# Storing layer 1's rows from SyncE in rank order and gathering them by rank in the batch norm's stage

## The chip, the cores and the metric

The kernel runs on one core of a Trainium2 chip. The metric is the device time of one execution in microseconds (us), from the first to the last instruction. Five engines work side by side, each on its own in-order list of instructions: TensorE (PE, matrix products), VectorE (DVE), ScalarE (ACT), GpSimd (POOL, which here does little but issue indirect DMAs) and SyncE (SP, which issues the plain DMAs).

## The reference

A graph of N = 2708 nodes with 128 features each, and a sparse weighted adjacency `adj` (about 0.6% of the entries and the diagonal), go through four layers. Each is `x = layernorm(x + layer(x, adj))`:

```
L0: (adj.T @ x) / column sums of adj
L1: s, d = x @ Ws.T, x @ Wd.T
    agg[i] = sum_j adj[i, j] * gelu(s[i] + d[j] + b)
    layernorm(gelu([x, agg] @ U.T + b) + x) * w + b
L2: h = adj @ (x @ W) + b;  batch norm over the nodes;  leaky relu
L3: 4 heads of GATv2 attention over adj, then a projection
```

What matters here: the result of layer 1, one row per node, is needed twice. Times W it goes into layer 2's product, and as it is it is added to layer 2's output after the batch norm (the residual).

## The kernel before

Layer 0 is one pass over `adj` in 22 blocks of 128 rows (the last has 20). The same pass finds each row's nonzero entries, counts them, and **ranks** the nodes by that count within two groups of blocks. From then on layer 1 works in rank order: a block holds 128 nodes of neighbouring rank, so that all need about the same number of neighbours (`CAPS`, 30 down to 8). Two tables translate: `rank[p, b]` is the rank of node 128b+p, and `perm[p, b]` is the node of rank 128b+p.

**Layer 1** takes the 22 blocks in the order `TURNS` (0 to 18, 21, 19, 20). For a block, `messages(b)` lets POOL gather one neighbour row per node and neighbour from `d_dram` (`gather`, L247; 368 gathers in all) into a `msg` tile of up to 8 neighbours (five such tiles in turn). DVE adds `s` (L896), ACT takes the gelu (L899), and DVE weighs and sums (L884) into `parts`. `update(b)` then runs a chain through PE, ACT and DVE (two layer norms) that ends in the block's finished rows `x_n` (written by `normalised`, L321). `x_n` goes two ways: it is transposed on PE (L937) and multiplied by W into `xw` (L941, L942), and it is **scattered** by `perm` to `x2_dram` in the nodes' natural order (L936, issued by POOL through `scatter`, L255; each waits also for the one before it, since all write one tensor).

In the first half of this stage, beside it, PE transposes `adj` (L969, L976) through SP into `at_dram`. In the second half, beside it, **layer 2** runs: `layer2(k)` gathers 128 whole rows of `at_dram` by `perm` (1.4 MB, POOL, `at_rows`) and multiplies them with `xw` of the block into six accumulators (L1018). Layer 2's output comes out in the nodes' natural order.

**The batch norm's stage** follows. It loads layer 1's rows `x2` from `x2_dram` (two plain loads on SP, L1103 and L1104), adds a shift to the accumulators (`hb`, L1129), sums the squares over the nodes with matmuls by ones (`ps_v`, L1132), makes `bn_scale` of that, and then per group of up to four blocks scales (L1185, L1186, L1187), adds `x2` (L1190), normalises into `x_nat` (L321), scatters these rows by `rank` to `x3_dram` (POOL, 22 scatters), and forms layer 3's table `t2_dram` with PE, ACT and SP (L1213 to L1232). Beside it `masks(g)` makes constants for layer 3: POOL writes index patterns (`jrow` L1147, `row_of` L1155, `start` L1157) and DVE turns them into `first`, `copies`, `alike`, `mask` and `same` (L1159 to L1179); three of the seven kinds stand in the program before the scaling, four after it.

**Layer 3** gathers rows of `t2_dram` (400 gathers on POOL) and works on them to the end.

The order of each engine's instructions is worked out when the program is built, by a planner that runs the program with estimated costs and, for each engine, takes the earliest instruction of the program that is ready; only layer 0's DVE work and layer 3's PE, DVE and ACT work have their order written out by hand. The planner also places every wait. The SBUF space of `x2` is free only when layer 2's last product has been read.

Of the kernel before, what the change touches and what calls it, by code (L numbers as in the profile page):

```python
# [15 lines left out]
P = 128  # L16
N = 2708
D = 128
NFULL = N // P
NREM = N - NFULL * P  # L20
NBLK = NFULL + 1
# [40 lines left out]
BLOCKS = [(b * P, min(P, N - b * P)) for b in range(NBLK)]  # L62
# [23 lines left out]
def gnn_resnorm_kernel(  # L86
# [21 lines left out]
    nc = tc.nc  # L108
# [108 lines left out]
    x2_dram = tables.tile([NBLK * P, D], FP, name="x2_dram")  # L217
# [6 lines left out]
    perm = keep.tile([P, NBLK], I32, name="perm")  # L224
# [7 lines left out]
    rank = keep.tile([P, NBLK], I32, name="rank")  # L232
# [9 lines left out]
    def natural(dram, b0, b1):  # L242

        return dram[b0 * P : b1 * P, :].rearrange("(b p) w -> p b w", p=P)

    def gather(dst, table, index):
        nc.gpsimd.indirect_dma_start(  # L247
            out=dst,
            out_offset=None,
            in_=table[0:N, :],  # L250
            in_offset=bass.IndirectOffsetOnAxis(ap=index, axis=0),
        )

    def scatter(table, index, rows):
        return nc.gpsimd.indirect_dma_start(  # L255
            out=table,
            out_offset=bass.IndirectOffsetOnAxis(ap=index, axis=0),
            in_=rows,
            in_offset=None,
        ).ins  # L260
# [35 lines left out]
    def deviation(small, n, count, h, sums, newton=True):  # L296


        var = small.tile([P, 4], FP, name="ln_var")
        junk = small.tile([P, D], BF, name="ln_junk")  # L300
        nc.vector.tensor_scalar(sums, sums, -1.0 / D, None, ALU.mult)
        for j in range(count):
            nc.scalar.activation(
                junk[0:n], h[:, j, :], AF.Square, bias=sums[:, j : j + 1],
                accum_out=var[0:n, j : j + 1],
            )
        v = var[0:n, 0:count]
        nc.vector.tensor_scalar(v, v, 1.0 / D, EPS, ALU.mult, ALU.add)
        if newton:
            for _ in rsqrt(small, n, count, v):  # L310
                pass
        else:
            nc.scalar.activation(v, v, AF.Sqrt)
            nc.vector.reciprocal(v, v)
        return var

    def normalised(small, n, count, h, sums, dst, newton=True):

        var = deviation(small, n, count, h, sums, newton)
        for j in range(count):  # L320
            nc.vector.tensor_scalar(  # L321
                dst[:, j, :], h[:, j, :], sums[:, j : j + 1], var[0:n, j : j + 1],
                ALU.add, ALU.mult,
            )
# [12 lines left out]
    with ExitStack() as layer:  # L337
# [568 lines left out]
        def update(b, x_s, x_st, parts):  # L906
            n = BLOCKS[b][1]
            tp = tail_ps.tile([P, 512], FP, name="tail")
            for i in range(2):
                nc.tensor.matmul(  # L910
                    tp[:, 0:n], lhsT=parts[0:n, i, :], rhs=ident[0:n, 0:n],
                    start=(i == 0), stop=(i == 1),
                )
            x_b = mine.tile([P, D], FP, name="x_b")
            nc.vector.tensor_tensor(x_b[0:n], x_s[0:n, 1, :], lnb[0:n], ALU.add)
            agg_t = mine.tile([P, P], FP, name="agg_t")
            nc.scalar.copy(agg_t[:, 0:n], tp[:, 0:n])
            pn = tp[0:n, P : 2 * P]
            nc.tensor.matmul(pn, lhsT=x_st[:, 0:n], rhs=u1_t, start=True, stop=False)
            nc.tensor.matmul(pn, lhsT=ones[0:1, 0:n], rhs=updb[0:1, :], start=False, stop=False)  # L920
            nc.tensor.matmul(pn, lhsT=agg_t[:, 0:n], rhs=u2_t, start=False, stop=True)
            new = mine.tile([P, 1, D], FP, name="new")
            x_n = mine.tile([P, 1, D], FP, name="x_n")
            sums = mine.tile([P, 2], FP, name="sums1")
            h, s0, s1 = new[0:n, 0, :], sums[0:n, 0:1], sums[0:n, 1:2]
            nc.scalar.activation(h, pn, AF.Gelu)
            nc.vector.scalar_tensor_tensor(
                h, h, 1.0, x_s[0:n, 1, :], ALU.mult, ALU.add, accum_out=s0
            )
            rstd = deviation(mine, n, 1, new[0:n], s0)  # L930
            nc.vector.scalar_tensor_tensor(h, h, s0, lnw[0:n], ALU.add, ALU.mult)
            nc.vector.scalar_tensor_tensor(
                h, h, rstd[0:n, 0:1], x_b[0:n], ALU.mult, ALU.add, accum_out=s1
            )
            normalised(mine, n, 1, new[0:n], s1, x_n[0:n])
            scatter(x2_dram, perm[0:n, b : b + 1], x_n[0:n, 0, :])  # L936
            nc.tensor.transpose(tp[:, 256 : 256 + n], x_n[0:n, 0, :], ident[0:n, 0:n])  # L937
            x_nt = mine.tile([P, P], FP, name="x_nt")
            nc.scalar.copy(x_nt[:, 0:n], tp[:, 256 : 256 + n])
            px = tp[0:n, 384:512]  # L940
            nc.tensor.matmul(px, lhsT=x_nt[:, 0:n], rhs=w2_l2, start=True, stop=True)  # L941
            nc.scalar.copy(xw[0:n, b, :], px)  # L942
# [92 lines left out]
        for i, b in enumerate(TURNS):  # L1035
# [10 lines left out]
            for _ in range(2 if i < 1 else 1):  # L1046
                if left:
# [6 lines left out]
                    if e == NBLK - 1:  # L1054
                        run(place(NBLK - 2, NBLK, lists(NBLK - 2, NBLK)))
            update(b, x_s, x_st, agg)
            if second and i:
                own_scatter(*second.pop(0))
# [39 lines left out]
    with ExitStack() as layer:  # L1098
# [1 line left out]
        small = layer.enter_context(tc.tile_pool(name="bn_small", bufs=2))  # L1100
        hb = work.tile([P, NBLK, D], FP, name="hb")
        x2 = work.tile([P, NBLK, D], FP, name="x2")
        nc.sync.dma_start(x2[:, 0:NFULL, :], natural(x2_dram, 0, NFULL))  # L1103
        nc.sync.dma_start(x2[0:NREM, NFULL, :], x2_dram[NFULL * P : N, :])  # L1104
        a_all = keep.tile([P, HEADS, D], FP, name="a_all")
        nc.scalar.dma_start(a_all, att.partition_broadcast(P))
        w1_sb = keep.tile([P, HEADS, D], FP, name="w1_s")
# [989 lines left out]
```

## Time and profile before

| | us |
|---|---|
| time, median of 3 runs | 1930.35 |
| the runs | 1926.28, 1930.35, 1936.67 |
| the profiled execution: its span | 1936.7 |
| layer 0 and the lists, about | 0 to 300 |
| layer 1, transposes beside it | 300 to 660 |
| layer 1, layer 2 beside it | 660 to 1033 |
| batch norm's stage | 1033 to 1117 |
| layer 3 | 1117 to 1937 |

The profiled execution's span, 1936.7 us, agrees with the slowest of the three runs, so it stands 6.3 us above the median. Busy over the whole span are PE 64%, DVE 60%, POOL 46% and ACT 40%. In the lines of the profile, "POOL L255 x_dram<-x_n,perm" is layer 1's scatter (buffer numbers are left out of names, so `x2_dram` and `x3_dram` both read `x_dram`), "L247" is a gather, and `[9.24 <-DVE x_n L321]` says that the engine stood idle for 9.24 us before this instruction and what ended the wait. "issue" is a wait that the profile doesn't explain by another engine.

### The profile page before, as it was taken

How to read it: one execution, taken by the hardware profiler on the slowest of the kernel's cores; microseconds unless marked ns; L12 is line 12 of the kernel's file. 1: busy time of each engine (PE TensorE's matmuls, PEld its weight loads, DVE VectorE, ACT ScalarE, POOL GpSimd, SP SyncE). 2: the span in 40 equal slices, each digit the busy share in tenths (PEclk: the TensorE clock that was granted, in tenths of full speed). 3: DMA queues.
4: the chain of work that ended last, by engine and by line, in shares of the span. 5: the costliest groups of instructions: out<-in, count | busy, mean ns of one | idle time of the engine just before them, and what ended most of it. 6: DMA issues, size and time to landing. Idle time of an engine off the chain costs nothing. (4 is left out here: it accounts for less than half of the span.)

```text
span 1936.7 us, 23643 instructions
## 1 busy us (share of the span) xinstructions
PE 1240.9 (64%) x5771; PEld 864.1 (45%) x5771; DVE 1166.6 (60%) x4895; ACT 776.5 (40%) x3156; POOL 892.8 (46%) x1003
## 2 busy tenths in 40 slices
PE   7974313353446553554673748888788788878885
PEld 7973212242334442554663314544444444444444
DVE  8997445675635423433447417777678677676774
ACT  3565345543324210211122415555455555445553
POOL 1004654445653366445331474655555556555430
PEclk9986555555555576776676756676676777666675
DMA  8642645666545525223231574865566655756540
GB/s 283 238 150 79 131 140 165 174 183 174 141 103 142 177 43 160 95 92 140 79 113 44 167 239 131 212 190 163 145 196 183 182 166 160 191 150 192 150 115 7
DMA packets 167676, 289.63 MB, mean 150 GB/s; under 512 B 49600, under 2 KB 121502, under 8 KB 160429
## 3 DMA queue, kind: packets, MB, share of 16 engines
q0 software_dynamic: 60496, 190.77, 34.4%
q1 hardware_dynamic: 99489, 92.57, 15.6%
q10 hardware_dynamic: 7544, 4.69, 1.0%
q8 instruction: 48, 0.79, 0.2%
q14 instruction: 99, 0.81, 0.1%
HBM read 242.51 MB, written 45.36 MB: 149 GB/s over the span
## 5 line engine op out<-in xcount | busy, mean ns | idle before, releaser
L247 POOL DMA_INDIRECT g<-t_dram,idx x400 | 398.6, 996 | 316.0 <-issue 178.9
L247 POOL DMA_INDIRECT msg<-d_dram,idx x368 | 348.6, 947 | 260.2 <-issue 164.8
L1389 ACT ACTIVATE sum_junk<-g 126x128 bf16<-126x128 f32 (+3 forms) x1024 | 301.3, 296 | 142.4 <-issue 59.8
L1358 PE MATMUL z<-x,copies 32*126 32x512 f32 (+3 forms) x800 | 221.3, 944 | 65.8 <-DVE g L1555 45.0
L969 PE MATMUL pt_a<-ident,rows 128*128 128x128 f32 (+2 forms) x475 | 114.1, 395 | 144.4 <-ACT at_sb L974 79.5
L1555 DVE TENSOR_TENSOR g<-g,z 126x1536 f32<-126x1536 f32 (+3 forms) x100 | 175.0, 1750 | 44.0 <-DMA g<-t_dram,idx 15.3
L1018 PE MATMUL acc<-x_nat,at_rows 128*128 128x128 f32 (+2 forms) x968 | 160.7, 326 | 52.3 <-DMA at_rows<-at_dram,perm 26.5
L1389 ACT ACTIVATION_READ_ACCUMULATOR sum_junk<-g 126x1 f32 (+3 forms) x1024 | 191.6, 187 | 0.0
L1018 PEld LDWEIGHTS acc<-x_nat,at_rows 128*128 128x128 f32 (+2 forms) x968 | 144.1, 232 | 65.5 <-issue 38.7
L1363 PE MATMUL z<-g,ident 126*126 126x512 f32 (+3 forms) x200 | 169.3, 941 | 0.7 <-issue 0.7
L1435 PE MATMUL po_s<-wm,g 126*128 126x24 f32 (+6 forms) x800 | 128.6, 316 | 58.5 <-DVE wm L1422 56.2
L1435 PEld LDWEIGHTS po_s<-wm,g 126*128 126x128 f32 (+3 forms) x800 | 124.8, 243 | 75.6 <-DVE wm L1422 67.9
L969 PEld LDWEIGHTS pt_a<-ident,rows 128*128 128x128 f32 (+2 forms) x475 | 82.9, 205 | 167.5 <-ACT at_sb L974 92.8
L884 DVE SCALAR_TENSOR_TENSOR own<-msg,ls,own 128x128 f32<-128x128 f32 (+1 forms) x302 | 105.6, 350 | 85.4 <-ACT msg L899 28.5
L1381 DVE SCALAR_TENSOR_TENSOR g<-g,a_ps 126x1536 f32<-126x1536 f32 (+6 forms) x100 | 151.0, 1510 | 0.0
L420 PE MATMUL acc<-x_nat,rows 128*128 128x129 f32 (+3 forms) x1012 | 128.5, 288 | 26.0 <-DMA rows<-in_adj_dram 14.9
L420 PEld LDWEIGHTS acc<-x_nat,rows 128*128 128x128 f32 (+2 forms) x1012 | 123.0, 198 | 31.2 <-DMA rows<-in_adj_dram 16.0
L1358 PEld LDWEIGHTS z<-x,copies 32*126 32x126 f32 (+3 forms) x800 | 67.8, 261 | 100.3 <-issue 46.5
L899 ACT ACTIVATE msg<-msg 128x896 f32<-128x896 f32 (+4 forms) x55 | 50.4, 917 | 132.9 <-DVE msg L896 92.1
L1373 DVE SCALAR_TENSOR_TENSOR g<-z,a 126x128 f32<-126x128 f32 (+3 forms) x400 | 91.9, 285 | 19.5 <-remote 9.2
L445 DVE FIND_INDEX8 ci<-cv,rows 128x8 uint32<-128x247 f32 (+2 forms) x242 | 98.7, 408 | 0.0
L1363 PEld LDWEIGHTS z<-g,ident 126*126 126x126 f32 (+3 forms) x200 | 42.0, 263 | 124.3 <-issue 117.3
(302 smaller groups left out, 2132.2 us busy)
## 6 DMA issues: line engine op xcount, KB each, us to landing
rows<-in_adj_dram SPq DMA_DIRECT2D x34, 1354.0 KB
at_dram<-at_sb SPq DMA_DIRECT2D x105, 256.0 KB
g<-t_dram,idx POOLq DMA_INDIRECT x400
msg<-d_dram,idx POOLq DMA_INDIRECT x368
t_dram<-t_row SPq DMA_DIRECT2D x21, 256.0 KB
x_s<-dx_dram SPq DMA_DIRECT2D x21, 128.0 KB
at_dram<-at_sb SPq DMA_DIRECT2D x21, 64.0 KB
t_dram<-x_nat SPq DMA_DIRECT2D x5, 256.0 KB
```

What stands on the lines that cost most here:

```text
L247: nc.gpsimd.indirect_dma_start(out=dst, out_offset=None, in_=table[0:N, :], in_offset=bass.IndirectOffsetOnAxis(ap=index, axis=0),)
L420: nc.tensor.matmul(accs0[k][0:m, c0 : c0 + f1 - f0], lhsT=rows[0:n, j0 : j0 + m], rhs=x_nat[0:n, b, f0:f1], start=k not in started, stop=( ...
L445: nc.vector.max_index(out=ci[0:n, at], in_max=cv[0:n, at], in_values=rows[0:n, c0 : c0 + cw])
L884: nc.vector.scalar_tensor_tensor(to, m, v, last, ALU.mult, ALU.add)
L969: nc.tensor.transpose(pt[0:m, j, 0:n], rows[0:n, c0 : c0 + m], ident[0:n, 0:n])
L1018: nc.tensor.matmul(accs2[ib // 4][0:m, (ib % 4) * D : (ib % 4 + 1) * D], lhsT=at[0:n, i0 : i0 + m], rhs=xw[0:n, b, :], start=(k == 0 and i ...
L1358: nc.tensor.matmul(z3[0:e, r, :] if r < 3 else z1[0:e], lhsT=copies[g][rows, j, :], rhs=own[b][1][rows, :], start=True, stop=r < 3, skip_g ...
L1363: nc.tensor.matmul(z1[0:e], lhsT=ident[0:e, 0:e], rhs=g4[0:e, 3, 0:HD], start=False, stop=True, skip_group_check=True,)
L1381: nc.vector.scalar_tensor_tensor(z, z, 0.0, a_ps[0:e].unsqueeze(1).to_broadcast((e, count, HD)), ALU.max, ALU.mult)
L1389: nc.scalar.activation(junk[0:e], g4[0:e, r, hd * D : (hd + 1) * D], AF.Identity, accum_out=sc[0:e, r, hd : hd + 1],)
L1435: nc.tensor.matmul(po[:, p0 * HEADS : (p0 + g) * HEADS], lhsT=g4s[i][0:e, r, HD : HD + D], rhs=wm[0:e, 4 * i + r, :, :], start=True, stop= ...
L1555: nc.vector.tensor_tensor(z, z, z3[0:e], ALU.add)
```

## The change

The 22 scatters of `x_n` are replaced by 22 plain stores from SP, block by block, so `x2_dram` holds the rows in rank order. In the batch norm's stage the two plain loads are replaced by 22 gathers on POOL, one per block of 128 nodes, that fetch by `rank`. What is computed is the same, and so are the bytes that are moved.

```diff
@@ update(b) in layer 1
             normalised(mine, n, 1, new[0:n], s1, x_n[0:n])
-            scatter(x2_dram, perm[0:n, b : b + 1], x_n[0:n, 0, :])
+            nc.sync.dma_start(x2_dram[b * P : b * P + n, :], x_n[0:n, 0, :])
             nc.tensor.transpose(tp[:, 256 : 256 + n], x_n[0:n, 0, :], ident[0:n, 0:n])
@@ the batch norm's stage
         hb = work.tile([P, NBLK, D], FP, name="hb")
         x2 = work.tile([P, NBLK, D], FP, name="x2")
-        nc.sync.dma_start(x2[:, 0:NFULL, :], natural(x2_dram, 0, NFULL))
-        nc.sync.dma_start(x2[0:NREM, NFULL, :], x2_dram[NFULL * P : N, :])
+        for b in range(NBLK):
+            n = BLOCKS[b][1]
+            gather(x2[0:n, b, :], x2_dram, rank[0:n, b : b + 1])
```

## The prediction

> **What bounds the kernel now.** I read the busy time by stage first, since the change touches two stages only.
>
> ```profile
> core 0: us, PE busy (x) PEld busy (x) DVE busy (x) ACT busy (x) POOL busy (x), PEclk, DMA share, GB/s
> 300.00:660.00 360.00, 160.99 (x650) 124.77 (x650) 201.60 (x1013) 141.41 (x297) 174.26 (x183) 0.55 0.56 147
> 660.00:1033.00 373.00, 213.30 (x1250) 185.60 (x1250) 143.55 (x613) 59.15 (x162) 169.75 (x180) 0.70 0.33 109
> 1033.00:1062.00 29.00, 7.55 (x48) 7.01 (x46) 26.44 (x90) 9.32 (x26) 1.89 (x11) 0.67 0.20 57
> 1062.00:1117.00 55.00, 39.00 (x114) 20.54 (x113) 26.13 (x144) 22.39 (x63) 23.50 (x27) 0.75 0.51 163
> ```
>
> No engine fills layer 1 (300 to 1033); its second half leans on PE (213 of 373). From 1033 to 1062 DVE is the bound (26.4 of 29), from 1062 on PE's chain. Second view: POOL's waits, 660 to 1033.
>
> ```profile
> POOL x_dram L255 <- DVE x_n L321: 67.1, 6, 16.5
> ...
> POOL x_dram L255 <- DVE own L884: 47.5, 5, 14.1
> POOL x_dram L255 <- DVE spread L618: 15.1, 1, 15.1
> ```
>
> So the scatter holds POOL for 129.7 us in 12 of the last blocks (from 300 to 660 never over 0.3 us). A hold costs only if something behind it is late. Message gathers are early: block 18's ran from 874 to 909 and DVE took the first at 926. Layer 2's `at_rows` gathers are not. Third view, the timelines of POOL and PE around 720:
>
> ```profile
> 717.83 1.00 POOL L255 DMA_INDIRECT x_dram<-x_n,perm  x1 [9.24 <-DVE x_n L321]
> 719.13 0.96 POOL L247 DMA_INDIRECT msg<-d_dram,idx  x1 [0.30 <-issue]
> ...
> 726.64 0.94 POOL L247 DMA_INDIRECT at_rows<-at_dram,perm  x1 [0.30 <-issue]
> ...
> 735.62 4.63 PE L1018 MATMUL acc<-x_nat,at_rows 128*128 128x128 f32 x25 [12.10 <-DMA at_rows<-at_dram,perm]
> ```
>
> POOL stands 9.24 us for `x_n`, then issues six message gathers, then `at_rows`; PE stands 12.10 us for it. Fourth view, DVE and POOL in the batch norm's stage:
>
> ```profile
> 1033.12 0.13 POOL L1147 IOTA jrow<- 128x8 int32 x1 [8.18 <-PE acc L1018]
> ...
> 1033.35 0.22 DVE L1159 TENSOR_SCALAR first<-jrow,in 128x8 f32<-128x8 int32 x1
> ...
> 1042.75 0.29 DVE L1142 TENSOR_SCALAR bn_scale<-ps_v 128x128 f32<-128x128 f32 x1 [2.49 <-PE ps_v L1132]
> ...
> 1044.14 1.87 DVE L1166 TENSOR_REDUCE alike<-copies 128x128 f32<-128x1024 f32 x1
> ...
> 1051.35 0.69 DVE L1185 TENSOR_TENSOR hb<-hb,bn_scale 128x512 f32<-128x512 f32 x1
> ```
>
> POOL's patterns are ready at once, so DVE makes masks ahead of the scaling, on the path.
>
> **Part 1, the scatters leave POOL.** Each took 1.00 us and 0.30 to the next, 22 x 1.30 = 28.6 us. In the first half messages are gathered some 30 us ahead of use (block 5's end at 442, DVE starts it at 473), and five message tiles stop POOL, not the scatter: 0. In the second half what counts is PE's waits for `at_rows`, 26.5 us in four: 4.95 before the first scatter that holds, which stays; 12.10 at 736; 6.18 at 811; 3.30 at 979. The scatters ahead of the last three held POOL 9.24, 3.20 and 15.09 us. Hold and scatter gone, each can shrink by the smaller of the two: 9.24 + 1.30 = 10.5, 3.20 + 1.30 = 4.5, and 3.3, together 18.3 us. PE is in order and carries this half, so a wait removed moves what follows; but chains through ACT and DVE can absorb some, and message tiles can stop POOL instead. Bounds 0 and 18.3; I take two thirds, 12 us, nearer the upper end because most of it is the one wait at 736.
>
> **Part 2, the stores on SP.** A 128 KB row load on SP (L857) mostly took 0.3 to 0.5 us to issue: 22 x 0.4 = 9 us on a queue that is empty for long stretches after 660, so 0 there. A store waits for `x_n`, and behind it in the first half stand `at_dram` stores; late ones hold the three `at_sb` tiles, ACT's copies behind them, and with ACT the gelu. ACT already waits 27.4 us on these stores (25 times, 4.7 at most) in layer 1. In the second half only `own_row` loads stand behind, which wait for a later step of the same chain. Bounds: 0, and 27 if those waits doubled; I take +2, since the planner puts the store where it expects `x_n`.
>
> **Part 3, 22 gathers in the batch norm's stage.** They can't start before 1033.1, when `x2`'s space comes free (the old load issued then too). At the message gathers' spacing, 0.94 + 0.30 = 1.25 us, POOL is held 22 x 1.25 = 27.5 us, to 1060.6. An indirect transfer is complete about 2.6 us after its start (two scatters of lists that wait for each other stand 2.6 apart, 463.29 and 465.88). So block b lands near 1033.1 + 1.25b + 2.6: block 3 at 1039.5, 11 at 1049.5, 21 at 1062. DVE added them at 1056.5, 1065.3 and 1088.9; 8 us earlier that would still be 1048, 1057 and 1081. All in time: the gathers themselves cost 0, and the removed loads gain 0, being hidden in the same way.
> A rule speaks against this part. The Trainium skill's "DMA: Bandwidth & Descriptors", section "Rules for kernel authors", says to join many small transfers into a large one, and its section on the anatomy of a GpSimd DMA gives about 2.0 us plus bytes over 436 GB/s for each. As an estimate from that page, one after another, 22 x 2.15 = 47 us would end at 1080, just at the last row's need. The 1.25 us spacing in this trace shows that they overlap, so the rows decide, and by the page too the sum would hardly change.
>
> What stands behind the gathers on POOL does move: the five patterns of 1033.1 to 1033.8 run at 1060.6 (the planner takes earlier instructions first, and the gathers are earlier). DVE's three masks, 11.5 us between 1033 and 1062 (L1162 4.19, L1166 4.70, the small ones 2.6), can't run there. If the planner fills in the scaling, it starts when the scale is ready: ACT's root ends at 1043.8, then 0.94 and 0.28 on DVE, 1045.05 instead of 1051.35, 6.3 us sooner; two further mask steps (1.7 us) before the first `x_nat` at 1061.4 make it 8 at most. I take -6. The 11.5 us go into 1062 to 1117, where DVE has 55 - 26 = 29 free, so they cost 0; without that cover they would cost 11.5. The 22 `x3_dram` scatters start at 1062 and end at 1096 now, then POOL idles 12.9 us to 1108.8: gathers to 1061 leave them where they are.
>
> One cost is unseen: `ps_v`'s 44 products (7.2 us, to 1042.7, on the path) will run beside indirect DMAs. Beside them PE's pace varies: 24 products in 2.84 us at 901, but 55 from 684 to 713 with POOL busy for 18.8 us, against 30 in 6 us right after, with POOL still. At 0.53 us each, 44 would take 23 us: +16; at the first pace 0. I take +3, nearer the low end, since at 684 the granted clock was low too (0.62).
>
> **Sum** against the profiled 1936.7: -12 + 2 - 6 + 3 = -13, 0.67%. On the median, 1930.35 x 0.9933 = 1917.
>
> **Rivals.**
> *The gain is absorbed.* Block times in layer 1 are set by PE, ACT and DVE handing over to one another, the `at_rows` waits become waits for message tiles, and part 3 balances. For it: ACT and DVE show waits of up to 27 us there that no scatter explains. Against it: the 12.1 us wait is plain. -13 + 12 = -1: about 1929.
> *Masks stall DVE (slower).* If the planner keeps a mask step where it stands on DVE, DVE waits in order for POOL's patterns behind 22 gathers. Place: `first<-jrow`, third on DVE at 1033.35, ahead of `hb`; price 1060.6 - 1033.3 = 27; if only those between 1042.95 and 1045.9 stay, 1060.6 - 1043 = 18. It decides as soon as any mask instruction stands ahead of the first L1185 on DVE. For it: they stand there now. Against it: the planner knows that POOL is held. Without part 3's -6: -12 + 2 + 3 + 18 to 27 = +11 to +20: 1941 to 1950.
> *POOL's freedom is worth more.* A quarter of the 129.7 us of holds, 32, instead of 12: 1897. Against it: message gathers are early.
>
> **How the numbers follow.** Forecast 0.45, absorbed 0.20, masks stall 0.25, more 0.10. The forecast's own range is 1904 (18.3 and 8 gained, neither +2 nor +3) to 1928 (half of part 1's, `ps_v` at +8). The range over the cases is 1893 to 1946, which cuts the ends of the outer two. About 0.5%, 10 us, is what this measurement can tell from no change. Faster by that: most of the forecast and all of "more", 0.50. Slower: the masks and a little of costlier SP waits or `ps_v`, 0.28. The rest 0.22.
>
> **What would show it.** Right: no x_dram<-x_n on POOL; PE's `at_rows` wait near 736 gone, layer 1 ending some 10 us sooner; 22 gathers back to back on POOL at the stage's start, L1185 about 12 us into it and no mask ahead of it; masks after 1062. Wrong: the stage still ending 84 us after its start or later, DVE idle with POOL's pattern as releaser; `ps_v` stretched over 10 us; SP waits on `x_n` with ACT's `at_sb` waits grown; layer 1 as long as before.

## The result, and the profile after

The changed kernel takes 1941.37 us (median of 20 runs, 1931.4 to 1956.09) against 1930.24 us of the kernel before (20 runs): a ratio of 1.0058, 95% interval 1.0041 to 1.0076. It is slower by 11 us. The profiled execution has a span of 1941.6 us against 1936.7. One thing has to be known for the numbers further down: the kernel before took 1917.47 us beside the first group of experiments and 1602.52 and 1601.93 beside the second and third, so ratios are compared within a group only.

Below, "the stage" starts when DVE writes `bn_mean` (end of layer 1). Four marks are counted from there: the first `x_nat` written, the last `t_row` copied, layer 3's first gather (POOL), and layer 3's first product on `g` (DVE). Behind the changed line, line numbers of the changed kernel are one higher than before: L1186 is the scaling that was L1185, L1160 is `first`, L1163 `copies`.

The first view is busy time by window, as before (length, then PE, PEld, DVE, ACT, POOL):

```profile
core 0: us, PE busy (x) PEld busy (x) DVE busy (x) ACT busy (x) POOL busy (x), PEclk, DMA share, GB/s
660.00:1024.00 364.00, 220.21 (x1202) 188.68 (x1202) 136.13 (x587) 56.46 (x158) 148.22 (x157) 0.69 0.30 95
1024.00:1053.00 29.00, 6.00 (x47) 5.35 (x46) 8.91 (x20) 5.34 (x9) 22.20 (x24) 0.68 0.21 57
1053.00:1130.00 77.00, 35.79 (x115) 19.07 (x115) 44.72 (x212) 26.48 (x81) 28.18 (x40) 0.74 0.38 119
```

Layer 1 ends 8.9 us earlier (1024.15, was 1033.07). PE's chain there no longer shows the wait of 12.10 us: in the stretch where PE stood (723.5 to 735.6) it now computes (its blocks come some 20 us sooner there), and over the span its group of `acc` waits 6.7 us for `at_rows` (26.5 before). The first line is from PE's timeline, the second from the groups of PE (busy, mean ns, idle before and what ended it):

```profile
724.45 7.81 PE L1018 MATMUL acc<-x_nat,at_rows 128*128 128x128 f32 x54
```

```profile
L1018 PE MATMUL acc<-x_nat,at_rows 128*128 128x128 f32 x882 | 151.9, 333 | 17.7 <-issue 10.4 <-DMA at_rows<-at_dram,perm 6.7 <-ACT x_nat L942 0.4
```

In the first 29 us of the stage DVE now works 8.9 us, where it worked 26.4; POOL is the one busy engine. The timeline of POOL and DVE in that stretch (start, duration, idle time before in brackets):

```profile
1024.38 0.95 POOL L247 DMA_INDIRECT x<-x_dram,rank  x1 [78.04 <-PE pw L1092]
...
1051.97 0.90 POOL L247 DMA_INDIRECT x<-x_dram,rank  x1 [0.30 <-issue]
1052.90 0.15 POOL L1148 IOTA jrow<- 128x8 int32 x1
```

```profile
1034.63 0.69 DVE L1186 TENSOR_TENSOR hb<-hb,bn_scale 128x512 f32<-128x512 f32 x1
1053.09 0.23 DVE L1160 TENSOR_SCALAR first<-jrow,in 128x8 f32<-128x8 int32 x1 [17.76 <-issue]
...
1064.05 0.69 DVE L1186 TENSOR_TENSOR hb<-hb,bn_scale 128x512 f32<-128x512 f32 x1
...
1069.57 1.11 DVE L321 TENSOR_SCALAR x_nat<-hb,sums,ln_var 128x128 f32<-128x128 f32 x4
```

The 22 gathers run back to back from 1024.38 to 1052.87. DVE issues one scaling, 10.5 us into the stage, and then stands 17.76 us. Its next instruction is the first mask step, which reads `jrow`, and POOL makes `jrow` at 1052.90, behind the last gather. The masks of three kinds then run ahead of nearly all of the quads' steps, and the first `x_nat` is written 45.4 us into the stage (28.4 before). The bracket only says "issue"; that POOL is the releaser follows from the times here, and three later runs name it. PE, which needs `x_nat`, stands 37.77 us:

```profile
1069.97 1.24 PE L1214 MATMUL pt_x<-ident,x_nat 128*128 128x128 f32 x4 [37.77 <-DVE x_nat L321]
...
1135.66 1.75 DVE L1556 TENSOR_TENSOR g<-g,z 128x1536 f32<-128x1536 f32 x1 [2.92 <-PE z L1359]
```

Layer 3's first product on `g` follows 111.5 us after the stage's start, 91.9 before. The balance of the two profiles: 8.9 us won in layer 1, 19.6 lost in the stage, 5.8 won in layer 3 (805.9 against 811.7, where the program is the same); -8.9 + 19.6 - 5.8 = +4.9 = 1941.6 - 1936.7. The medians differ by 11.1; the profiled execution of the kernel before, at 1936.7, is slower than its median. A difference of 6 us between two single profiles thus proves nothing by itself.

### The profile page after: what moved, and what is told of

The parts are those of the page before. It is cut to its first block, busy times and chain, and to the rows that moved or that the text cites. A ratio compares the mean times of both kernels' runs of the same rounds, so it can differ in the third digit from the quotient of the medians.

```text
span 1941.6 us, 23697 instructions
## 1 busy us (share of the span) xinstructions
PE 1238.7 (64%) x5771; PEld 864.5 (45%) x5771; DVE 1165.8 (60%) x4895; ACT 774.2 (40%) x3156; POOL 895.8 (46%) x1003
## 5 line engine op out<-in xcount | busy, mean ns | idle before, releaser
L1359 PE MATMUL z<-x,copies 32*126 32x512 f32 (+3 forms) x800 | 212.5, 910 | 53.8 <-DVE g L1556 32.8
L1556 DVE TENSOR_TENSOR g<-g,z 126x1536 f32<-126x1536 f32 (+3 forms) x100 | 175.0, 1750 | 34.0 <-remote 19.9
L1018 PE MATMUL acc<-x_nat,at_rows 128*128 128x128 f32 (+2 forms) x968 | 169.5, 335 | 17.7 <-issue 10.4
L1018 PEld LDWEIGHTS acc<-x_nat,at_rows 128*128 128x128 f32 (+2 forms) x968 | 150.6, 239 | 32.6 <-issue 27.2
L420 PE MATMUL acc<-x_nat,rows 128*128 128x129 f32 (+3 forms) x1012 | 129.5, 289 | 26.5 <-DMA rows<-in_adj_dram 15.5
L1359 PEld LDWEIGHTS z<-x,copies 32*126 32x126 f32 (+3 forms) x800 | 63.9, 251 | 86.4 <-issue 46.1
L1374 DVE SCALAR_TENSOR_TENSOR g<-z,a 126x128 f32<-126x128 f32 (+3 forms) x400 | 91.9, 286 | 17.2 <-issue 13.1
L450 DVE MAX8 cv<-rows 128x8 f32<-128x247 f32 (+2 forms) x242 | 95.6, 401 | 2.4 <-POOL rows L410 2.4
```

The costliest lines, as they stand in the source:

```text
L420: nc.tensor.matmul(accs0[k][0:m, c0 : c0 + f1 - f0], lhsT=rows[0:n, j0 : j0 + m], rhs=x_nat[0:n, b, f0:f1], start=k not in started, stop=( ...
L1018: nc.tensor.matmul(accs2[ib // 4][0:m, (ib % 4) * D : (ib % 4 + 1) * D], lhsT=at[0:n, i0 : i0 + m], rhs=xw[0:n, b, :], start=(k == 0 and i ...
L1359: nc.tensor.matmul(z3[0:e, r, :] if r < 3 else z1[0:e], lhsT=copies[g][rows, j, :], rhs=own[b][1][rows, :], start=True, stop=r < 3, skip_g ...
L1556: nc.vector.tensor_tensor(z, z, z3[0:e], ALU.add)
```

## The experiments

Theory A: layer 1's stores gain what the trace shows, and the loss is DVE waiting in its own order for patterns that POOL makes behind the gathers. Rivals: the gathers themselves cost (D), or layer 1's gain is lost elsewhere (B). All runs in a table; the marks are us after the stage's start. The expectations of group 1 count the stage to layer 3's first gather: 84.4 before, 103.5 changed. The first product on `g` comes 7.5 to 8.1 us later.

| kernel | group | ratio to before (95%) | stage's start | first `x_nat` | last `t_row` | layer 3's first gather | first product on `g` |
|---|---|---|---|---|---|---|---|
| before (first profile) | | 1 | 1033.07 | 28.4 | 78.2 | 84.4 | 91.9 |
| changed (first profile) | | 1.0058 (1.0041 to 1.0076) | 1024.15 | 45.4 | 97.2 | 103.5 | 111.5 |
| stores_alone | 1 | 0.9914 (0.988 to 0.9948) | 1004.44 | 28.4 | 73.1 | 79.1 | 86.6 |
| gathers_alone | 1 | 1.01 (1.0066 to 1.0135) | 1016.80 | 45.3 | 93.8 | 99.7 | 107.6 |
| patterns_first | 1 | 1.0003 (0.9971 to 1.0034) | 1006.77 | 40.3 | 87.7 | 93.7 | 101.7 |
| masks_last | 1 | 0.995 (0.9911 to 0.9989) | 1006.05 | 20.5 | 78.3 | 84.4 | 92.4 |
| patterns_own | 2 | 0.9877 (0.9849 to 0.9904) | 806.62 | 27.0 | 65.0 | 71.2 | 79.3 |
| half_gathers | 2 | 0.9856 (0.9819 to 0.9892) | 811.63 | 33.6 | 71.8 | 78.1 | 86.0 |
| one_kind_first | 2 | 0.9904 (0.9876 to 0.9932) | 808.14 | 37.9 | 77.4 | 83.5 | 91.5 |
| before_masks_last | 2 | 0.996 (0.9939 to 0.9981) | 832.51 | 22.9 | 62.5 | 68.7 | 76.1 |
| before_again | 3 | a single run, 1595.56 us | 824.78 | 28.3 | 67.1 | 73.2 | 80.7 |
| after_again | 3 | 0.9989 (0.9966 to 1.0013) | 807.39 | 45.2 | 88.7 | 94.7 | 102.7 |
| patterns_own_2 | 3 | 0.9838 (0.9807 to 0.9869) | 810.04 | 28.3 | 67.3 | 73.5 | 81.5 |
| split_patterns | 3 | 0.9838 (0.9818 to 0.9857) | 806.77 | 23.0 | 68.7 | 74.7 | 82.8 |

### The two halves, each alone

`stores_alone` is the changed kernel with the old loads:

```
-        for b in range(NBLK):
-            n = BLOCKS[b][1]
-            gather(x2[0:n, b, :], x2_dram, rank[0:n, b : b + 1])
+        nc.sync.dma_start(x2[:, 0:NFULL, :], natural(x2_dram, 0, NFULL))
+        nc.sync.dma_start(x2[0:NREM, NFULL, :], x2_dram[NFULL * P : N, :])
```

> Layer 1 as in the changed kernel (SyncE stores x_n in rank order), the batch norm's stage as before: x2 by the two plain loads, so the rows are added in rank order; leaving out the gathers is what the run is for. Theory A (the stores save some 9 us by the end of layer 1, 1033.07 to 1024.15, and the 22 gathers lose 19 in the next stage, 84.4 to 103.5): the stage keeps its 84 us, layer 3 begins near 1108.5 instead of 1117.5, and the time is 9 below before: 1921 (1917 to 1925). Rival B (layer 1's gain is given back later whatever the gathers do): 1928 to 1932. Rival C (the stage's longer time comes from the early end of layer 1, not from the gathers): the stage again takes over 95 us, 1935 or more.

`gathers_alone` is the kernel before with the opposite edit.

> The other half: layer 1 keeps the scatters on POOL, and the batch norm's stage reads x2 with the 22 indirect DMAs. x2 is in natural order here, so the gathers fetch rows by rank from the wrong places; their count, size and indices are those of the changed kernel. Theory A: layer 1 ends near 1033, DVE waits about 18 us for POOL's first pattern behind the gathers, the stage takes 101 to 105 us, and the time is before plus 19: 1949 (1944 to 1954). Rival B (the gathers cost little by themselves, the loss needs the change in layer 1): under 1936. Rival C (layer 1's gain is real and the gathers cost only the +11 of the whole change, layer 1's gain being lost elsewhere): 1941.

Measured: -0.86% and +1.00%. The first profile's signs come back in separate kernels. In the same group layer 1 ends 12.4 us earlier with the stores than with the scatters (1004.44 against 1016.80), and the first `x_nat` comes 28.4 us into the stage with the loads, 45.3 with the gathers, as in the two first profiles. Layer 3's first gather comes at 79.1 us with the loads (84 expected) and at 99.7 with the gathers (101 to 105 expected). In `gathers_alone` too the wait stands at the first mask:

```profile
1028.63 0.69 DVE L1186 TENSOR_TENSOR hb<-hb,bn_scale 128x512 f32<-128x512 f32 x1
1045.59 0.23 DVE L1160 TENSOR_SCALAR first<-jrow,in 128x8 f32<-128x8 int32 x1 [16.27 <-issue]
```

The first ratio is lower than theory A asked (0.993 at least), in part since layer 1 won more than 9 us here. Rivals B and C fall: the stores are worth something by themselves, and the gathers cost without them.

### The patterns ahead of the gathers

`patterns_first` moves the gathers behind the masks in the program:

```
         for g in KINDS[:3]:
             masks(g)
+        for b in range(NBLK):
+            n = BLOCKS[b][1]
+            gather(x2[0:n, b, :], x2_dram, rank[0:n, b : b + 1])
```

> The changed kernel with the loop of 22 gathers written behind the masks of the first three kinds instead of at the head of the stage, so that POOL makes jrow, row_of and start before the gathers. Same work, another order on POOL. Theory A (DVE's 17.76 us at the first mask are a wait for POOL's order and nothing else): no idle time of DVE over 3 us ends at a pattern, the masks run ahead of the scaling as before, where the stage took 84.4 us; the gathers begin some 8 us later and the last lands about 36 us into the stage, beyond the 23 us at which before first needed x2, so the last quads may wait a little: stage 84 to 90 us, time 1921 to 1927. Rival D (the gathers themselves hold the stage back: their DMAs and POOL's 28 us, whatever is queued behind them): the stage stays over 97 us and the time at 1936 to 1943.

Measured 1.0003, layer 3's first gather 93.7 us into the stage: theory A's 84 to 90 is missed, and so is rival D's 97 or more. The timeline of DVE in this kernel shows why:

```profile
1020.96 1.25 DVE L1160 TENSOR_SCALAR copies<-row_of,first 128x125 f32<-128x125 int32 x6
...
1035.96 1.07 DVE L1160 TENSOR_SCALAR copies<-row_of,first 128x126 f32<-128x126 int32 x5 [11.81 <-issue]
...
1047.10 1.11 DVE L321 TENSOR_SCALAR x_nat<-hb,sums,ln_var 128x128 f32<-128x128 f32 x4
```

Two kinds' masks run early, and DVE stands 11.81 us at the third. `row_of` has two buffers, so POOL could write the third kind's only once the first kind's `same` had read its own, 13.8 us into the stage, and by then the 22 gathers were ahead in POOL's order. In the kernel before, POOL waited for the same release, with no gathers in the way:

```profile
1047.02 0.14 POOL L1157 IOTA start<- 128x6 int32 x1 [13.18 <-DVE mask L1175]
```

The wait had moved. `patterns_own` takes that reason away:

```
-            row_of = small.tile([P, e], I32, ..., tag="row_of", bufs=2)
+            row_of = small.tile([P, e], I32, ..., tag="row_of", bufs=3)
...
-            start = small.tile([P, g], I32, ..., tag="start", bufs=2)
+            start = small.tile([P, g], I32, ..., tag="start", bufs=3)
```

> As patterns_first, and row_of and start get three buffers each instead of two, so that the third kind's patterns need not wait for the first kind's masks (same[g], 13.8 us into the stage) and POOL makes all seven patterns ahead of the gathers. In patterns_first the wait had only moved: DVE stood 11.81 us at the third kind's copies, whose row_of came behind the gathers, and the first x_nat was written 40.3 us into the stage. Theory A (the loss is DVE's wait in order behind POOL's gathers): no such wait is left, the first x_nat comes 28 to 30 us into the stage, as before (28.4), layer 3's first product on g follows 90 to 94 us after the stage's start, as before (91.9), and only layer 1's gain of 9 to 12 us is left: 0.990 to 0.995 of the time before. Rival D (the gathers themselves cost, by their DMAs and 28 us of POOL): first x_nat over 34 us in, 0.998 to 1.006.

Measured 0.9877. DVE's timeline:

```profile
822.45 1.09 DVE L1160 TENSOR_SCALAR copies<-row_of,first 128x126 f32<-128x126 int32 x5
823.54 0.68 DVE L1186 TENSOR_TENSOR hb<-hb,bn_scale 128x512 f32<-128x512 f32 x1
...
833.65 1.11 DVE L321 TENSOR_SCALAR x_nat<-hb,sums,ln_var 128x128 f32<-128x128 f32 x4
```

The same 22 gathers run, but no mask waits, and the first `x_nat` comes 27.0 us into the stage. Rival D falls. The ratio is a little below what theory A allowed, and the first product on `g` comes at 79.3 us, not 90 to 94: `before_again` further down shows that the kernel before takes 80.7 us to this mark under these conditions.

### The size of the wait, and what it takes to have it

`masks_last` leaves the gathers at the head of the stage and moves the masks:

```
-        for g in KINDS[:3]:
-            masks(g)
         for b0, count, n in quads():
...
-        for g in KINDS[3:]:
+        for g in KINDS:
             masks(g)
```

> The changed kernel with the first three kinds of masks written behind the quads with the others, the gathers at the head of the stage. DVE has no mask ahead of the scaling. Theory A: scaling starts 10.5 us into the stage and goes on from quad to quad, x2's rows landing every 1.3 us ahead of it; the first x_nat comes 18 to 22 us into the stage (45.4 in the changed kernel, 28.4 before). POOL's scatters of x3 wait for the gathers' end, 28 us in, and the masks (11.5 us of DVE) stand at the end, under the last copies or in front of layer 3. Stage 76 to 86 us, time 1913 to 1923. Rival D (the gathers hold the stage back by themselves): over 97 us and 1936 to 1943. Rival E (the masks then hold up layer 3's start instead): stage 86 to 95 us, 1923 to 1933.

Measured 0.995, inside theory A's range, and so are the marks: the first `x_nat` comes at 20.5 us, layer 3's first gather at 84.4. Rival D falls by its numbers, rival E (86 to 95) narrowly. But `stores_alone` in the same group takes 79.1 us to this mark, so that being early on DVE bought nothing here. DVE's timeline:

```profile
1037.19 0.42 DVE L301 TENSOR_SCALAR sums<-sums 128x4 f32<-128x4 f32 x1 [5.56 <-remote]
...
1046.35 0.19 DVE L301 TENSOR_SCALAR sums<-sums 128x4 f32<-128x4 f32 x1 [4.79 <-remote]
```

DVE, now early, stands twice inside the quads. What released it ("remote") the trace doesn't name. Late rows of `x2` are an unlikely reason: the waiting instruction reads only `sums`, which DVE writes, and in `split_patterns` below DVE adds the fourth quad's second row block 27 us into the stage without such a wait, here at 31. Idle time under "remote" is 242 us on DVE over this whole run, 181 to 242 in the other profiles of the first pair and of group 1, and 0.0 in all eight of groups 2 and 3. So the two waits may belong to the conditions of the group; they stay open.

`half_gathers` gathers 11 blocks and loads the other 11 plainly:

> The changed kernel with the first 11 blocks of x2 gathered and the other 11 read by the two plain loads (these rows come in rank order, so part of the re-ordering is left out). Theory A: POOL reaches jrow 11 x 1.25 = 13.8 us earlier, 15 us into the stage; the first mask starts there instead of at 28.9, the first x_nat comes 13 to 15 us earlier (31 to 33 us in, from 45.4), and the ratio to before falls by 13.8 of 1930, from 1.0058 to 0.997 to 1.000. Rival F (the 22 scatters of x3 on POOL or the DMA traffic set the stage's length, and the wait at the masks hides in it): first mask early, but layer 3's start moves by under 5 us and the ratio stays over 1.002.

```profile
825.63 0.23 DVE L1162 TENSOR_SCALAR first<-jrow,in 128x8 f32<-128x8 int32 x1 [6.01 <-POOL jrow L1150]
```

Here the trace names POOL's `jrow` as what DVE waits for, 14.0 us into the stage instead of 28.8. The first `x_nat` comes 11.6 us earlier than in the changed kernel of group 3, which ran beside the same 1602 us (33.6 against 45.2; 13 to 15 expected), layer 3 16.7 us earlier. So half the gathers make about half the hold, and rival F falls. The ratio, 0.9856, lies further below than theory A said: group 3 shows that the changed kernel itself stands at 0.9989 here, not 1.0058, which makes 13.3 thousandths or 21 us for a step of 13.8. Some 10 us of it come after the stage and are unexplained.

`one_kind_first` puts only the first kind's masks ahead of the gathers:

```
+        for g in KINDS[:1]:
+            masks(g)
+        for b in range(NBLK):
+            n = BLOCKS[b][1]
+            gather(x2[0:n, b, :], x2_dram, rank[0:n, b : b + 1])
...
-        for g in KINDS[3:]:
+        for g in KINDS[1:]:
             masks(g)
```

> The changed kernel with only the first kind's masks written ahead of the 22 gathers, the other six kinds behind the quads. DVE's order then has one single instruction of the second kind (a copies of 0.28 us) ahead of the scaling, and its row_of stands behind the gathers on POOL. Theory A (one waiting instruction ahead on an engine that goes in order costs the whole wait): DVE idles 10 to 14 us at this one instruction, from 15 to 29 us into the stage, and the first x_nat is written 34 to 38 us in; 0.998 to 1.003 of before. Rival H (the stall needs the whole block of masks ahead of the scaling; one instruction of 0.28 us costs little): first x_nat 20 to 26 us in, 0.990 to 0.995.

```profile
820.69 0.28 DVE L1143 TENSOR_TENSOR bn_scale<-bn_scale,gamma_row 128x128 f32<-128x128 f32 x1
837.25 0.43 DVE L1160 TENSOR_SCALAR copies<-row_of,first 128x125 f32<-128x125 int32 x1 [16.28 <-POOL row_of L1153]
837.45 1.29 DVE L1186 TENSOR_TENSOR hb<-hb,bn_scale 128x512 f32<-128x512 f32 x2
```

The scale is ready at 820.97. One `copies` instruction of the second kind, which nothing on the way to `x_nat` needs, stands ahead of the scaling in DVE's order, its `row_of` comes from POOL behind the gathers, and DVE idles 16.28 us. Rival H falls: one such instruction costs the whole wait. (By the ratio alone, 0.9904, rival H would stand: its range was 0.990 to 0.995. The ratio is below theory A's for the reason given above, and since two kinds' masks no longer stand in front of the quads. The first `x_nat` at 37.9 us and the wait decide.)

`before_masks_last` makes the same move of the masks in the kernel before:

> The kernel before with the first three kinds of masks written behind the quads, as in masks_last; scatters in layer 1 and plain loads of x2 as they were. It shows what the masks' place alone is worth. Theory A (masks_last gains from the masks' place what the gathers cost, and both are separate): scaling starts some 3 us earlier than before, the first x_nat comes 20 to 25 us into the stage, the masks return later under other work or in front of layer 3: 0.996 to 1.001 of before. Rival G (the place of the masks is worth the whole of masks_last's gain): 0.990 to 0.995.

Measured 0.996 (0.9939 to 0.9981), first `x_nat` 22.9 us in, first product on `g` 4.6 us sooner than in `before_again`: the place of the masks alone is worth 0.4%. That is nearly all of the 0.5% of `masks_last`, and the interval reaches into rival G's range, so rival G isn't excluded. But `masks_last` has layer 1's stores too, which alone are worth 0.9%: some 0.8% is missing in it, and its first product on `g` comes 5.8 us later than that of `stores_alone` (92.4 against 86.6). In that kernel the gathers cost time with no mask ahead of the scaling; why is not shown.

### The same conditions for all, and a better version

> The changed kernel once more, unchanged, beside the kernels of this group: the second group ran in some 1600 us where the first took 1917 for the same kernel before, so that the size of the loss in microseconds has to be seen again under these conditions. Theory A (a loss of 17 to 19 us in the batch norm's stage less a gain of layer 1 that was 9 us at 1930 and, by the shorter times of the second group, is 12 or more): the stage's wait at the first mask again lasts 17 to 19 us, the first x_nat comes 44 to 46 us into the stage; in all 0.996 to 1.006 of before. Rival B (the wait shrinks with the rest): under 12 us and below 0.995.

> The kernel before, unchanged, for a profile beside those of this group. Theory A: first x_nat 27 to 29 us into the stage, as in the first profile (28.4), since nothing there waits for POOL; end of layer 1 later than in the changed kernel by 9 to 20 us. Rival: the stage is itself shorter by over 4 us here, and what was read in the second group against 28.4 has to be read anew.

In group 3 the changed kernel is at 0.9989, an interval that holds 1. The wait at the first mask lasts 16.2 us (17 to 19 expected). The rival of `before_again` holds: to the first product on `g` the kernel before takes 80.7 us here, 11.2 less than in the first profile, all of it behind the first `x_nat`. DVE's wait in the changed kernel first, then PE's waits in layer 1 of the kernel before and of the changed one (us in total, times, longest):

```profile
DVE first L1160 <- POOL jrow L1148: 16.2, 1, 16.2
```

```profile
PE acc L1018 <- DMA at_rows<-at_dram,perm: 75.3, 8, 26.5
```

```profile
PE acc L1018 <- DMA at_rows<-at_dram,perm: 44.0, 7, 10.0
```

The loss keeps its size: first `x_nat` 45.2 against 28.3 us, layer 3's mark 102.7 against 80.7. The gain is larger here: PE waits 31.3 us less for `at_rows`, and layer 1 ends 17.4 us earlier (807.39 against 824.78). With -17.4 + 22.0 and the rest of the program 2.4 us longer, the two profiles differ by +7.0 (the single run of `before_again` is faster than all 17 of the kernel before beside it); over the runs the two kernels are alike. The loss is 16.9 us at the first `x_nat` and 22.0 at the product on `g`. The rest fits a second wait of DVE, at a mask of the last kind whose pattern POOL makes between the scatters of `x3`:

```profile
883.85 0.16 DVE L1172 TENSOR_SCALAR_CACHE_REDUCE after<-start 128x10 f32<-128x10 int32 x1 [5.23 <-POOL start L1158]
```

Where in layer 1 the gain arises can be read from the times at which DVE writes a block's `x_n` (L321):

| `x_n` written, in order | before | changed | sooner by | before_again | after_again | sooner by |
|---|---|---|---|---|---|---|
| 1st | 328.1 | 325.1 | 3.0 | 274.6 | 274.4 | 0.2 |
| 10th | 652.1 | 637.1 | 14.9 | 534.0 | 532.9 | 1.1 |
| 12th | 717.2 | 686.9 | 30.3 | 576.3 | 574.6 | 1.7 |
| 13th | 741.6 | 722.8 | 18.8 | 592.6 | 594.4 | -1.8 |
| 17th | 899.7 | 899.6 | 0.0 | 715.1 | 710.5 | 4.6 |
| 22nd | 1023.3 | 1014.8 | 8.5 | 814.8 | 798.0 | 16.7 |

In group 3 the gain comes in the second half, where the waits for `at_rows` shrank. In the first profiles it does not follow the wait of 12.10 us: 30 us were there before that wait, and all were gone at the 17th block. So the trace of the first pair does not show by which path its 8.9 us came.

`split_patterns` splits `masks(g)`: POOL's patterns of three kinds stand ahead of the gathers, DVE's part behind the quads.

```
+        for g in KINDS[:3]:
+            patterns(g)          # row_of, start; bufs=3
+        for b in range(NBLK):
+            n = BLOCKS[b][1]
+            gather(x2[0:n, b, :], x2_dram, rank[0:n, b : b + 1])
...
-        for g in KINDS[3:]:
+        for g in KINDS:
             masks(g)
```

> The changed kernel with the patterns of three kinds (jrow, row_of, start, three buffers) made by POOL ahead of the gathers, and the masks that DVE makes of them written behind the quads: DVE can then fill idle time with masks but has none to wait for. It joins patterns_own (no wait behind the gathers) and masks_last (no mask in front of the scaling). Theory A: no wait of DVE at a mask, first x_nat 19 to 24 us into the stage, x2's rows arrive 1.25 us apart and hold up the quads from the third on (blocks 9 on land after 14 us); stage 72 to 80 us, 0.983 to 0.989 of before, at or below patterns_own. Rival I (scatters of x3 on POOL set the stage's end: they can begin only behind the last gather, 29 us in, and take 28 us): as patterns_own within 2 us.

> patterns_own once more, beside the changed kernel and split_patterns in one group. Theory A: 0.985 to 0.992 of before, and 16 to 20 us below the changed kernel, which is DVE's wait at the first mask. Rival: within 8 us of the changed kernel.

Both are at 0.9838 and beat both kernels: 1576.34 and 1578.74 us against 1601.93 before and 1600.85 for the change as it was made. `patterns_own_2` is 22 us below the changed kernel (16 to 20 expected). Against `before_again` it shows what the change is worth without the wait: layer 1 ends 14.7 us earlier, the stage takes 81.5 us against 80.7, so that 22 gathers on POOL cost 0.8 us in this order.

`split_patterns` writes its first `x_nat` 5.3 us sooner and gains nothing from it: layer 3's first gather comes at 74.7 us, 73.5 in `patterns_own_2`. That is nearly the time of rival I, but the trace shows another cause. Theory A's "no wait of DVE at a mask" failed. The timelines of POOL, DVE and PE:

```profile
835.46 0.94 POOL L247 DMA_INDIRECT x<-x_dram,rank  x1 [0.30 <-DMA x<-x_dram,rank]
836.96 1.34 POOL L255 DMA_INDIRECT x_dram<-x_nat,rank  x1 [0.18 <-DMA x<-x_dram,rank]
...
864.42 0.26 POOL L1154 IOTA row_of<- 128x126 int32 x1
```

```profile
864.71 0.93 DVE L1170 TENSOR_SCALAR copies<-row_of,first 128x126 f32<-128x126 int32 x3 [4.19 <-POOL row_of L1154]
...
866.64 0.15 DVE L1240 COPY beta_t<-pa_t 128x4 f32<-128x4 f32 x1
```

```profile
866.85 0.59 PE L1234 MATMUL pa_t<-w_a,xt 128*128 128x4 f32 x2 [4.92 <-DVE beta_t L1240]
```

The masks now run late and keep the three `row_of` buffers, so POOL makes the later kinds' patterns only between and behind the scatters of `x3`. DVE stands 2.41 and 4.19 us for them, its copy `beta_t` stands behind that, and PE stands 4.92 us for `beta_t`, in the chain that makes layer 3's table. It is the cost of the change once more, in another place, and about the 5.3 us that were won.

Rival I said that the scatters set the stage's end. In all 14 profiles layer 3's first gather comes 5.9 to 6.3 us after the last `t_row`, but 11.9 to 22.4 us after the last scatter's start. So the table's chain ends the stage, and POOL's row of DMAs counts through the patterns in it. Nor are the gathers free in this order: `before_masks_last`, with the masks in the same place and no gathers, reaches the first product on `g` at 76.1 us, `split_patterns` at 82.8.

## Why the prediction was wrong

The forecast was 1917, faster by 0.67%; the runs say slower by 0.58%, inside the range but on the other side. Step by step:

- **Part 1, the scatters leave POOL (-12): right in sign and size, the path shown in group 3 only.** The step was that PE's waits for `at_rows`, 26.5 us in four, shrink by up to 18.3. They are 6.7 us in the changed kernel, and the 12.10 us at 736 is gone; the stage starts 8.9 us sooner in the first profile, 12.4 between two kernels of group 1, 17.4 in group 3. That a part is absorbed was in the step. In group 3 the waits shrink by 31.3 us and the gain comes where they stood; in the first profiles the lead over the blocks does not follow the wait at 736.
- **Part 2, the stores on SP (+2): too small to see.** ACT's waits before `at_sb` for the `at_dram` stores went from 28.8 to 32.4 us in the first profiles and from 66.4 to 54.9 in group 3, with no one sign (27.4 in the prediction counts layer 1 alone).
- **Part 3, the gathers and `x2` (0): right.** They were issued 1.25 us apart over 28.5 us (27.5 forecast), and in the order of `patterns_own_2` they cost 0.8 us. The price of the Trainium skill's "DMA: Bandwidth & Descriptors" that was weighed here is about 2 us for each DMA by its section on the anatomy of a GpSimd DMA, an estimate of 47 us one after another. The row of gathers was issued in 28.5 us; the measurement decides.
- **`ps_v` beside them (+3): not there.** Its 44 products took 5.99 us from first to last, 7.43 before. The slow pace that it was weighed by, 55 products in 29 us, was misread: by the view of busy time PE worked for 10.26 of these 29 us and stood for the rest. The low clock there (0.62) was no reason either; in the 6 us right after, with 30 products, it was 0.54.
- **Part 3, the masks (-6): this step failed.** It saw that the patterns would come behind the gathers, and it made this a gain by "if the planner fills in the scaling". The order on DVE had one scaling filled in and then the masks, ahead of the rest of the first quad. In place of -6 stands a wait of 17.76 us, with all three masks still in front: the stage took 19.6 us more. With +19.6 for the terms of the stage (-6 and +3), the sum is -12 + 2 + 19.6 = about +10, and the runs say +11. That the two meet so closely is luck: in group 3 the loss of the stage is as large, layer 1 gains more, and the two kernels are alike. The reading under this step was incomplete too: "POOL's patterns are ready at once" holds for two kinds, while the third kind's were made at 1047.02 in the kernel before, when a buffer came free.
- **The rival "Masks stall DVE"** named the mechanism, its price (18, the lower of the two) and the time (1941 to 1950; 1941.4 measured). Its argument against, that the planner knows that POOL is held, carried the chance and was wrong. Its point of decision was a little too narrow: no mask stood ahead of the first L1185, only ahead of the second and of the quad's other steps, and that was enough. `one_kind_first` shows how little is needed.

A cost that hangs on an "if" about an engine's order deserves both its values in the sum's range and a reason for the choice; here the one was -6, the other near +20, and the rows of before (masks ahead of the scaling) stood for the second.

## What to carry to other kernels

When DMAs are moved to an engine that also makes small inputs for others, look at what stands behind them there, and who will wait for it in order: 28 us of issue that cost 0.8 us in one order cost 20 in another, because a 0.15 us pattern came behind them. Make such patterns ahead of the queue, and give them a buffer each, or the buffers' release puts them behind it again (`patterns_first`, and `split_patterns` for the later kinds). An instruction that nobody needs yet is not harmless at the head of an in-order engine.

## What the runs showed of the hardware

- The same program ran in about 1930, 1917 and 1602 us. DVE's instructions last the same: its `g` products take 1750 ns on average in `before` and 1748 in `before_again`. PE's are shorter in the faster run: the `z` products (L1358) take 944 and 876 ns, at a mean granted clock of 0.667 and 0.718, and PE is busy for 1241 and 1160 us. Most of the difference of 343 us is idle time: DVE stands 230 us under "remote" and 105 under "issue" in `before`, 0.0 and 0.2 in `before_again`. The runs don't show where this comes from. It changed the gain in layer 1 (8.9 against 17.4 us) and hardly the wait in the stage (17.8 against 16.2).
- 22 indirect gathers of 64 KB left POOL 1.25 us apart, with one of 2.15 us among them, and beside them 44 products for `ps_v` took 0.14 us each (5.99 us in all), no more than without (7.43). In the other profiles with gathers they took 5.95 to 7.48 us.
